# Talking-heads attention with a soft mixture of experts: raw logits and head mixing on sixteen 32x32 array tiles, rows brought together by SBUF-to-SBUF DMAs

## The chip, the cores and the metric

The kernel runs on one core of one Trainium2 chip. The metric is the time of one execution on the device, in microseconds (us). The time before is the median of three runs; the profile is that of one further execution. TensorE (PE in the profile) does matmuls out of SBUF into PSUM; VectorE (DVE) and ScalarE (ACT) read PSUM; GpSimd (POOL) works on SBUF alone; SyncE (SP) here only issues DMAs. PEld is TensorE's loading of weights.

## The reference

Input x is (4, 2048, 256), all in float32. For each of the 4 batches:

```
q, k, v = split(x @ Wqkv.T + bqkv)             # 16 heads of 16
q, k = rope(q), rope(k)
s = q @ k.T / 4                                # per head: raw logits, 2048 x 2048
l[g] = sum over h of Wpre[g, h] * s[h]         # the heads are mixed
a = softmax(l over keys)
t[g] = sum over h of Wpost[g, h] * a[h]        # and mixed again
x = layernorm(x + (t @ v) @ Wout.T + bout)
x = layernorm(x + soft_moe(x))                 # 16 experts of 16 slots, 64 hidden
```

Nearly all of the time lies in the four lines from s to t @ v.

## The kernel before

The batches follow one another. For each, `qkv(b)` projects the 16 token tiles of 128 tokens and leaves q and k transposed in `qT` and `kT` (128 partitions, 2 chunks of 8 heads x 16, 2048 tokens) and v as rows. Then `attention` runs, then `moe`.

`attention` takes queries in pairs of blocks: a block x is 8 tokens, so a row of logits (token, head) fills one of 128 partitions, and a pair n holds 16 tokens. There are 128 pairs per batch, 512 in all. Keys are taken in two halves j of 1024. The steps of a pair:

- `block_q` (L340) spreads q over the heads with a mask, on GpSimd: `qb`, one instruction per pair.
- `raw_bank` (L357) makes the raw logits s of a bank of PSUM (128 x 512) with matmuls of 128 rows by 32 columns, four side by side (L368), and has the bank copied to `raw` in SBUF by DVE or ACT (L375). There are four banks per half.
- `logits` (L377) mixes the heads with Wpre, on four 64x64 tiles of the array (L389), into two PSUM tiles l of 1024 columns, one per block.
- `top` (L400) reduces l to its negated maximum m on DVE (L402); `expo` (L406) makes e = exp(l + m) with its sum on ACT (L410).
- `weights` (L416) corrects for the two halves' maxima: f and z on GpSimd, a short exponential of f on ACT (L424), a reciprocal of z on DVE (L429), and the scaled Wpost w on GpSimd (L432).
- `mix` (L442), four per pair in the next step of the loop, multiplies e with w and so transposes it (t, L461) into two banks each, copied to `aT` (L470) by DVE and ACT.
- `values` (L477) multiplies with v (o, L485), and `finish` (L503) projects with Wout (pz, L509) for every 128 tokens.

The loop over n writes out by hand what is interleaved: in step n the l of pair n, the s of pair n + 1, the mixes of pair n - 1. Each engine works through its instructions in the program's order. On TensorE that is, per step: l of half 0, s of half 0, mixes 1 and 2, l of half 1, mixes 3 and 4, s of half 1, o. On ACT the second half's order is: exponential, two copies of mix 3, exponential, f, one copy of mix 4, two copies of s; on DVE: two reductions, m, the other copy of mix 4, reciprocal z, two copies of s.

[...] The pool `ps_l` holds two tiles l of two banks; the pool `ps_t` has four single banks, which s, t, o and pz take in turn, 17 of them per pair. A bank is free again when it has been copied out. In SBUF the tag `raw` has 5 buffers (of 4 KB per partition), `k1` 6, `x` 4.

## Time and profile before

| what | value |
|---|---|
| median of three runs | 10,239.89 us (10,237.3 to 10,248.01) |
| the profiled execution, its own time | 10,242.24 us |
| its span in the profile | 10,240.5 us |
| mean granted TensorE clock | 0.986 of full speed |
| s, L368: 32,768 passes of 512 columns | 3,739.1 us busy |
| l, L389: 16,384 passes of 512 columns | 2,070.1 us busy |
| t, L461: 131,072 passes of 64 columns | 2,183.9 us busy |
| o, L485: 65,536 passes of 64 columns | 1,018.0 us busy |
| m, L402 on DVE: 2,048 reductions of 1024 | 2,412.7 us busy |
| e, L410 on ACT: 2,048 exponentials of 1024 | 2,285.8 us busy |
| all DMA | 74.04 MB, 63,584 packets |

A matmul of float32 appears as two passes, each with its own weight load. Busy times of one engine overlap where array tiles run side by side, so that a mean duration is longer than the distance of two passes. The chain of work that ended last follows the end of the program back from what released each step to what released that; its shares tell where time was spent that nothing else hid. The views by time (timeline, chain in order of time) give the start in us from the start of the span, the length, the engine, the line and the tile; a bracket holds the idle time ahead and what ended it. "Idle before, releaser" in the groups is the same, summed.

### The profile page before, as it was taken

Reading aid. Unit: us, or ns where it says so; the run is one execution under the profiler, and the core shown is the slowest. Engines: PE = TensorE matmul, PEld = TensorE weight load, DVE = VectorE, ACT = ScalarE, POOL = GpSimd, SP = SyncE. Lnnn points to the kernel's source line nnn. Section 1 sums busy time; section 2 is a strip of 40 time slices with the busy share of each in tenths; the row PEclk is TensorE's granted clock in tenths of the full one; section 3 lists DMA queues with packets and bytes.
Section 4 is the critical chain, followed back from the end, with each engine's and each line's share of the span. In section 5 each row is a group of like instructions: output and inputs, shape, how many; then the busy total and the mean of one; then the engine's idle time right before and its main releaser. Section 6 shows DMA issues by size and latency. Waiting matters only on the chain.

```text
span 10240.5 us, 523545 instructions
## 1 busy us (share of the span) xinstructions
PE 9268.5 (91%) x248404; PEld 5008.8 (49%) x248404; DVE 5613.3 (55%) x9064; ACT 4995.1 (49%) x9766; POOL 1284.9 (13%) x3409
## 2 busy tenths in 40 slices
PE   8999999997899999999689999999968999999996
PEld 4445545444444445445444545444544444444454
DVE  5555555554555555555455555555545555555554
ACT  3555555553455555555345555555534555555553
POOL 2111111111211111111121111111112111111111
PEclk9999999998999999999899999999989999999998
DMA  0000000000000000000000000000000000000000
GB/s 23 5 5 5 4 5 5 5 4 17 19 5 5 5 4 5 5 5 4 17 19 5 5 5 4 5 5 5 4 17 18 5 5 5 4 5 5 4 4 18
DMA packets 63584, 74.04 MB, mean 7 GB/s; under 512 B 30080, under 2 KB 59904, under 8 KB 61440
## 3 DMA queue, kind: packets, MB, share of 16 engines
q8 instruction: 1946, 31.88, 1.3%
q1 hardware_dynamic: 26880, 25.18, 0.8%
q10 hardware_dynamic: 34560, 15.36, 0.6%
q14 instruction: 198, 1.62, 0.1%
HBM read 32.13 MB, written 8.39 MB: 4 GB/s over the span
## 4 chain that ended last, share of the span: by engine, by line
PE 80%; ACT 9%; DVE 8%; issue 2%; POOL 1%; ACTq 0%; DMA 0%; POOLq 0%; DVEq 0%
PE s L368 36%; PE l L389 19%; PE t L461 10%; PE o L485 9%; DVE m L402 6%; ACT e L410 5%; ACT aT L470 3%; PE pqk L289 1%; PE pz L509 1%; PE pf L680 1%; PE l_d L197 1%; PE o_d L236 1%; POOL xn L591 0%; PE pv L294 0%; POOL xn L592 0%
## 5 line engine op out<-in xcount | busy, mean ns | idle before, releaser
L368 PE MATMUL s<-kT,qb 128*32 128x512 f32 x32768 | 3739.1, 596 | 551.4 <-ACT aT L470 551.3
L402 DVE TENSOR_REDUCE m<-l 128x1 f32<-128x1024 f32 x2048 | 2412.7, 1220 | 1269.8 <-PE l L389 1269.8
L410 ACT ACTIVATE e<-l,m 128x1024 f32<-128x1024 f32 x2048 | 2285.8, 1121 | 1262.7 <-DVE m L402 1262.6
L375 ACT COPY raw<-s 128x512 f32<-128x512 f32 x2048 | 1211.7, 592 | 2809.0 <-PE s L368 2808.4
L461 PEld LDWEIGHTS t<-w,e 64*64 64x64 f32 x131072 | 2103.4, 135 | 754.0 <-issue 685.9
L368 PEld LDWEIGHTS s<-kT,qb 128*32 128x32 f32 x32768 | 966.7, 109 | 2886.8 <-issue 1797.2
L461 PE MATMUL t<-w,e 64*64 64x64 f32 x131072 | 2183.9, 219 | 43.0 <-issue 34.9
L389 PE MATMUL l<-raw,wmix_sb 64*64 64x512 f32 x16384 | 2070.1, 596 | 7.2 <-ACT e L410 3.6
L470 ACT COPY aT<-t 128x512 f32<-128x512 f32 x2560 | 1450.4, 589 | 396.2 <-PE t L461 395.8
L375 DVE COPY raw<-s 128x512 f32<-128x512 f32 x2048 | 1354.7, 681 | 350.3 <-PE s L368 349.6
L470 DVE COPY aT<-t 128x512 f32<-128x512 f32 x1536 | 1058.2, 689 | 338.2 <-PE t L461 338.0
L485 PEld LDWEIGHTS o<-aT,v 128*32 128x32 f32 x65536 | 997.0, 110 | 329.3 <-issue 176.8
L485 PE MATMUL o<-aT,v 128*32 128x64 f32 x65536 | 1018.0, 220 | 31.6 <-issue 26.5
L423 POOL TENSOR_TENSOR f<-m,m 128x4 f32<-128x4 f32 x512 | 101.6, 198 | 6568.8 <-DVE m L421 6568.8
L389 PEld LDWEIGHTS l<-raw,wmix_sb 64*64 64x64 f32 x16384 | 566.5, 133 | 679.6 <-issue 616.8
L429 DVE RECIPROCAL z<-z 128x2 f32<-128x2 f32 x512 | 85.1, 166 | 1081.5 <-POOL z L428 1081.5
L496 DVE COPY aoT<-o 128x32 f32<-128x32 f32 x512 | 98.1, 192 | 1005.9 <-PE o L485 1005.7
L410 ACT ACTIVATION_READ_ACCUMULATOR e<-l,m 128x1 f32 x2048 | 421.9, 206 | 0.0
L343 POOL TENSOR_TENSOR qb<-qT,hmask 128x256 f32<-128x256 f32 x512 | 313.6, 634 | 73.3 <-PE s L368 73.3
L432 POOL TENSOR_TENSOR w<-wblk_sb,f 128x256 f32<-128x256 f32 x512 | 313.7, 613 | 40.3 <-POOL f L430 0.5
L426 POOL TENSOR_TENSOR zf<-f,z 128x4 f32<-128x4 f32 x512 | 102.5, 200 | 987.2 <-ACT f L424 987.2
L315 POOL TENSOR_TENSOR s<-qk,wq 128x256 f32<-128x256 f32 x128 | 115.9, 924 | 478.4 <-DVE qk L299 478.4
(123 smaller groups left out, 2602.0 us busy)
## 6 DMA issues: line engine op xcount, KB each, us to landing
x<-in_x_dram SPq DMA_DIRECT2D x64, 128.0 KB
xr<-in_x_dram SPq DMA_DIRECT2D x64, 128.0 KB
out_dram<-y SPq DMA_DIRECT2D x16, 512.0 KB
wm<-in_w_dram ACTq DMA_DIRECT2D x8, 512.0 KB
wm<-in_w_dram ACTq DMA_DIRECT2D x4, 1024.0 KB
wq<-in_wqkvT_dram ACTq DMA_DIRECT2D x4, 768.0 KB
wq<-in_bqkv_dram ACTq DMA_DIRECT2D x4, 384.0 KB
wq<-in_rope_dram ACTq DMA_DIRECT2D x4, 256.0 KB
```

The lines of the kernel that those rows point to most:

```text
L315: nc.gpsimd.tensor_mul(s[:, :, a, :], qk[:, :, 1 - a, :], ss[a])
L343: nc.gpsimd.tensor_tensor(qb, qT[:, :, ts(n, 2 * IB)].unsqueeze(3).to_broadcast([P, KC, 2 * IB, HC]), hmask.unsqueeze(1).unsqueeze(1).to_b ...
L368: nc.tensor.matmul(pr[32 * c : 32 * (c + 1), :], qb[:, c % 2, i0 : i0 + IQ, :].rearrange("p i h -> p (i h)"), kT[:, c % 2, j0 : j0 + 512], ...
L375: eng(raws[n][j, u][:, ts(jj, 512)], pr)
L389: nc.tensor.matmul(pls[x][64 * u : 64 * (u + 1), n0 : n0 + 512], wmix_sb[64 * x : 64 * (x + 1), :], raws[n][j, u][64 * x : 64 * (x + 1), n ...
L402: nc.vector.tensor_reduce(s["m2"][:, x, j : j + 1], s["l", j][x], AX.X, ALU.max, negate=True)
L410: nc.scalar.activation(e, s["l", j][x], AF.Exp, bias=s["m2"][:, x, j : j + 1], accum_out=s["z2"][:, x, j : j + 1],)
L426: nc.gpsimd.tensor_tensor(zf, f, z2, ALU.mult)
L432: nc.gpsimd.tensor_tensor(w, wblk_sb.rearrange("p g i -> p (g i)").unsqueeze(1).to_broadcast([P, 4, HEADS * IQ]), f.rearrange("p x j -> p ...
L461: nc.tensor.matmul(pts[r][64 * c : 64 * (c + 1), a, :], e[rows, k0 : k0 + 64], s["w"][rows, 2 * x + j, :], start=True, stop=True,)
L470: engs[r](aT[grp][:, ts(j, HT), :, i0 : i0 + IQ], pts[r].rearrange("p a (g i) -> p a g i", i=IQ),)
L485: nc.tensor.matmul(po[32 * c : 32 * (c + 1)].rearrange("p a i -> p (a i)"), v[:, t, g0 * HD : (g0 + 2) * HD], at[:, t, g0 : g0 + 2, :].rea ...
```

## The change

The raw logits go to sixteen 32x32 tiles: a row group of 32 partitions of q and k holds two heads, four column groups take the four 256-key quarters of the half, so that each PSUM bank belongs to one row group and holds both chunks of heads. A row of the array's output is then no longer a (token, head) row of one key range: partitions hold 32 combinations of key quarter, block, token and head parity, and the free axis holds 8 head pairs by 256 keys. Eight DMAs per key half, each with 16 partitions as source and 128 as destination, bring this into rows (token, head), with tokens arranged so that Wpre is applied on sixteen 32x32 tiles as well, which lie on diagonals of the array. All four banks of a half are filled by one call, chunk by chunk, and copied after that. `qb` is made by seven smaller instructions. `y` takes over the room of `qT`, `uT` that of `kT`, and the x tiles have two buffers.

```diff
-    RAWS = 5
+    RAWS = 3
+    ROWS = 6
+    HP = HEADS // 2
+    QN = 256
...
-        xt = work.tile([P, D], F32, tag="x", name=f"{name}_{b}_{t}", bufs=4)
+        xt = work.tile([P, D], F32, tag="x", name=f"{name}_{b}_{t}", bufs=2)
...
-        def block_q(n):
-
-            qb = k1([P, KC, 2 * IB, HC], f"qb_{b}_{n}")
-            nc.gpsimd.tensor_tensor(
-                qb,
-                qT[:, :, ts(n, 2 * IB)].unsqueeze(3).to_broadcast([P, KC, 2 * IB, HC]),
-                hmask.unsqueeze(1).unsqueeze(1).to_broadcast([P, KC, 2 * IB, HC]),
-                ALU.mult,
-            )
+        def pair_q(n):
+            qb = k1([P, KC, 2, 2, 4, 2, 2], f"qb_{b}_{n}")
+            t, t0 = divmod(n * 2 * IB, P)
+            for g in range(2):
+                for x in range(2):
+                    d = 2 * x + g
+                    for s0, s1 in ((0, 4 - d), (4 - d, 4)):
+                        if s0 == s1:
+                            continue
+                        i0 = t0 + x * IB + (s0 + d) % 4 * 2
+                        i1 = i0 + (s1 - s0) * 2
+                        shape = [P, KC, i1 - i0, 2]
+                        nc.gpsimd.tensor_tensor(
+                            qb[:, :, g, x, s0:s1].rearrange("p c s i h -> p c (s i) h"),
+                            qT[:, t, :, i0:i1].unsqueeze(3).to_broadcast(shape),
+                            hmask.unsqueeze(1).unsqueeze(1).to_broadcast(shape),
+                            ALU.mult,
+                        )
             return qb
...
-        def raw_bank(n, j, k, eng):
-            u, jj = k % 2, k // 2
+        def raw_banks(n, j, engs):
             qb = raws[n]["qb"]
-            pr = ps_t.tile([P, 512], F32, tag="t", name=f"s_{b}_{n}_{j}_{k}")
-            j0 = j * HALF + jj * 512
-            for c in range(4):
-                i0 = IB * (c // 2) + IQ * u
-                nc.tensor.matmul(
-                    pr[32 * c : 32 * (c + 1), :],
-                    qb[:, c % 2, i0 : i0 + IQ, :].rearrange("p i h -> p (i h)"),
-                    kT[:, c % 2, j0 : j0 + 512],
-                    start=True,
-                    stop=True,
-                )
-            eng(raws[n][j, u][:, ts(jj, 512)], pr)
+            prs = [
+                ps_t.tile([P, KC, QN], F32, tag="t", name=f"s_{b}_{n}_{j}_{r}") for r in range(4)
+            ]
+            for c in range(KC):
+                for r in range(4):
+                    rows = slice(32 * r, 32 * (r + 1))
+                    for q in range(4):
+                        nc.tensor.matmul(
+                            prs[r][32 * q : 32 * (q + 1), c, :],
+                            qb[rows, c, q // 2].rearrange("p x s i h -> p (x s i h)"),
+                            kT[rows, c, j * HALF + q * QN : j * HALF + (q + 1) * QN],
+                            start=True,
+                            stop=True,
+                        )
+            raw = raws[n]["from", j].rearrange("p (c r) k -> p c r k", c=KC)
+            return [lambda r=r: engs[r](raw[:, :, r, :], prs[r]) for r in range(4)]
+
+        def raw_rows(n, j):
+            raw, rows = raws[n]["from", j], raws[n]["to", j]
+            for q in range(4):
+                for x in range(2):
+                    p0 = 32 * q + 16 * x
+                    nc.sync.dma_start(rows[x][:, ts(q, QN)], raw[p0 : p0 + 16])
...
-            for n0 in range(0, HALF, 512):
-                for u in range(2):
-                    for x in range(2):
+            for x in range(2):
+                for h in range(2):
+                    for q in range(4):
+                        c = (q + 2 * x + h) % 4
                         nc.tensor.matmul(
-                            pls[x][64 * u : 64 * (u + 1), n0 : n0 + 512],
-                            wmix_sb[64 * x : 64 * (x + 1), :],
-                            raws[n][j, u][64 * x : 64 * (x + 1), n0 : n0 + 512],
+                            pls[x][32 * c : 32 * (c + 1), ts(h, 512)],
+                            wmix_sb[32 * q : 32 * (q + 1), :],
+                            raws[n]["to", j][x][32 * q : 32 * (q + 1), ts(h, 512)],
                             start=True,
                             stop=True,
                         )
...
-        uT = seq.tile([P, KC, N], F32, tag="qT", name=f"uT_{b}")
+        uT = seq.tile([P, KC, N], F32, tag="kT", name=f"uT_{b}")
...
-        y = seq.tile([P, NT, D], F32, tag="y", name=f"y_{b}")
+        y = heads[0].rearrange("p t c i -> p t (c i)")
```

In the program that comes out of this, TensorE keeps its order of blocks. On ACT a step now reads: two exponentials, two copies of s, two copies of mixes 1 and 2; two exponentials, two copies of mix 3, f, one copy of mix 4, two copies of s. On DVE: two reductions, two copies of s, two copies of mixes 1 and 2; two reductions, m, reciprocal z, the copy of mix 4, two copies of s. GpSimd makes qb behind w, several pairs ahead where its buffers allow. SyncE issues the sixteen DMAs of a pair, eight after each half's copies, with the x loads of `finish` among them. The first copy of a half waits for the eight DMAs that read its `raw` buffer three halves earlier.

More of the change, by code (lines that the diff above doesn't have):

```diff
@@ L78, in row_const @@
         return t
-    wmix_sb = const.tile([P, IQ * HEADS], F32, tag="wmix", name="wmix_sb")
+    wmix_sb = const.tile([P, 2 * HEADS], F32, tag="wmix", name="wmix_sb")
     nc.gpsimd.memset(wmix_sb, 0.0)
-    wpre_h = wpre.rearrange("(h d) g -> h d g", d=HD)
-    for r in range(P // HC):
-        c, i = divmod(r % (KC * IQ), IQ)
+    wpre_h = wpre.rearrange("(r a d) g -> a r d g", a=2, d=HD)
+    for r in range(P // HP):
+        i, h = divmod(r % 4, 2)
         nc.scalar.dma_start(
-            wmix_sb[r * HC : (r + 1) * HC, i * HEADS : (i + 1) * HEADS],
-            wpre_h[c * HC : (c + 1) * HC, 0, :],
-        )
-    hmask = const.tile([P, HC], F32, tag="hmask", name="hmask")
-    nc.gpsimd.memset(hmask, 1.0)
-    nc.gpsimd.affine_select(
-        out=hmask, in_=hmask, compare_op=ALU.is_ge, fill=0.0,
-        base=0, pattern=[[-HD, HC]], channel_multiplier=1,
-    )
-    nc.gpsimd.affine_select(
-        out=hmask, in_=hmask, compare_op=ALU.is_ge, fill=0.0,
-        base=HD - 1, pattern=[[HD, HC]], channel_multiplier=-1,
-    )
+            wmix_sb[r * HP : (r + 1) * HP, i * HEADS : (i + 1) * HEADS], wpre_h[h, :, 0, :]
+        )
     wblk_sb = const.tile([P, HEADS, IQ], F32, tag="wblk", name="wblk_sb")
@@ L113 @@
     scale_sb = row_const(scale, 1, "scale_sb")
-    mu_sb = work.tile([P, KC, ES], F32, tag="raw", name="mu_sb", bufs=RAWS)
+    mu_sb = work.tile([P, KC, ES], F32, tag="rows", name="mu_sb", bufs=ROWS)
     nc.scalar.dma_start(mu_sb, mu.rearrange("(c p) e -> p c e", p=P))
@@ L143 @@
     nc.vector.tensor_reduce(odd1, odd4, AX.X, ALU.max)
+    hmask = const.tile([P, 2], F32, tag="hmask", name="hmask")
+    nc.vector.tensor_scalar(hmask[:, 0:1], odd1, -1.0, 1.0, ALU.mult, ALU.add)
+    nc.vector.tensor_copy(hmask[:, 1:2], odd1)
     odd = const.tile([P, GI], mybir.dt.int32, tag="odd", name="odd")
     nc.vector.tensor_copy(odd, odd1.to_broadcast([P, GI]))
-    sq = work.tile([P, KC, ES], F32, tag="raw", name="sq", bufs=RAWS)
+    sq = work.tile([P, KC, ES], F32, tag="rows", name="sq", bufs=ROWS)
     nc.vector.tensor_mul(sq, mu_sb, mu_sb)
@@ L179, in k2 @@
     def k2(shape, name):
-        return work.tile(shape, F32, tag="raw", name=name, bufs=RAWS)
+        return work.tile(shape, F32, tag="rows", name=name, bufs=ROWS)
     def evac(i, dst, src):
@@ L274, in qkv @@
         nc.scalar.dma_start(rope_sb, rope.rearrange("(t p) k -> p t k", p=P))
-        qT = seq.tile([P, KC, N], F32, tag="qT", name=f"qT_{b}")
+        qT = seq.tile([P, NT, KC, P], F32, tag="qT", name=f"qT_{b}")
         kT = seq.tile([P, KC, N], F32, tag="kT", name=f"kT_{b}")
@@ L322, in turn @@
                 nc.tensor.transpose(pr[:, c, :], r[:, ts(c, P)], ident)
-            nc.vector.tensor_copy(qT[:, :, ts(t, P)], pr[:, :KC, :])
+            nc.vector.tensor_copy(qT[:, t], pr[:, :KC, :])
             nc.scalar.copy(kT[:, :, ts(t, P)], pr[:, KC:, :])
@@ L338, in attention @@
         raws = {}
-        def block_q(n):
-            qb = k1([P, KC, 2 * IB, HC], f"qb_{b}_{n}")
-            nc.gpsimd.tensor_tensor(
-                qb,
-                qT[:, :, ts(n, 2 * IB)].unsqueeze(3).to_broadcast([P, KC, 2 * IB, HC]),
-                hmask.unsqueeze(1).unsqueeze(1).to_broadcast([P, KC, 2 * IB, HC]),
-                ALU.mult,
-            )
+        def pair_q(n):
[16 more added lines that the diff above has]
+                        )
             return qb
@@ L352, in raw_start @@
             if j == 0:
-                raws[n] = {"qb": block_q(n)}
-            for u in range(2):
-                raws[n][j, u] = work.tile([P, HALF], F32, tag="raw", name=f"raw_{b}_{n}_{j}_{u}", bufs=RAWS)
-        def raw_bank(n, j, k, eng):
-            u, jj = k % 2, k // 2
-            qb = raws[n]["qb"]
-            pr = ps_t.tile([P, 512], F32, tag="t", name=f"s_{b}_{n}_{j}_{k}")
-            j0 = j * HALF + jj * 512
-            for c in range(4):
-                i0 = IB * (c // 2) + IQ * u
-                nc.tensor.matmul(
-                    pr[32 * c : 32 * (c + 1), :],
-                    qb[:, c % 2, i0 : i0 + IQ, :].rearrange("p i h -> p (i h)"),
-                    kT[:, c % 2, j0 : j0 + 512],
-                    start=True,
-                    stop=True,
-                )
-            eng(raws[n][j, u][:, ts(jj, 512)], pr)
+                raws[n] = {"qb": pair_q(n)}
@@ new lines, in raw_start @@
+            raws[n]["from", j] = work.tile([P, HP, QN], F32, tag="raw", name=f"raw_{b}_{n}_{j}", bufs=RAWS)
+            raws[n]["to", j] = [
+                work.tile([P, HALF], F32, tag="rows", name=f"rows_{b}_{n}_{j}_{x}", bufs=ROWS)
+                for x in range(2)
+            ]
+        def raw_banks(n, j, engs):
+            qb = raws[n]["qb"]
+            prs = [
+                ps_t.tile([P, KC, QN], F32, tag="t", name=f"s_{b}_{n}_{j}_{r}") for r in range(4)
+            ]
+            for c in range(KC):
[11 more added lines that the diff above has]
+            return [lambda r=r: engs[r](raw[:, :, r, :], prs[r]) for r in range(4)]
@@ L385, in logits @@
             pls = [ps_l.tile([P, HALF], F32, tag="l", name=f"l_{b}_{n}_{j}_{x}") for x in range(2)]
-            for n0 in range(0, HALF, 512):
-                for u in range(2):
-                    for x in range(2):
+            for x in range(2):
+                for h in range(2):
+                    for q in range(4):
+                        c = (q + 2 * x + h) % 4
                         nc.tensor.matmul(
-                            pls[x][64 * u : 64 * (u + 1), n0 : n0 + 512],
-                            wmix_sb[64 * x : 64 * (x + 1), :],
-                            raws[n][j, u][64 * x : 64 * (x + 1), n0 : n0 + 512],
+                            pls[x][32 * c : 32 * (c + 1), ts(h, 512)],
+                            wmix_sb[32 * q : 32 * (q + 1), :],
+                            raws[n]["to", j][x][32 * q : 32 * (q + 1), ts(h, 512)],
                             start=True,
@@ L518, in attention @@
             raw_start(0, j)
-            for k in range(4):
-                raw_bank(0, j, k, (V, S_)[k % 2])
+            for f in raw_banks(0, j, (V, S_, V, S_)):
+                f()
+            raw_rows(0, j)
         for n in range(n_pairs + 3):
@@ L525, in attention @@
             val = 0 <= grp < N // GI
+            nop = [lambda: None] * 4
             for j in range(2):
@@ L531, in attention @@
                 if j == 0:
-                    if nxt:
-                        raw_bank(n + 1, j, 0, S_)
+                    fs = raw_banks(n + 1, j, (S_, V, S_, V)) if nxt else nop
+                    fs[0]()
                     if cur:
@@ L536, in attention @@
                         expo(n, j, 0)
-                    if nxt:
-                        raw_bank(n + 1, j, 1, V)
+                    fs[1]()
                     if cur:
                         top(n, j, 1)
-                    if nxt:
-                        raw_bank(n + 1, j, 2, S_)
+                    fs[2]()
                     if cur:
                         expo(n, j, 1)
+                    fs[3]()
                     if nxt:
-                        raw_bank(n + 1, j, 3, V)
+                        raw_rows(n + 1, j)
                     if prv:
@@ L562, in attention @@
                     if nxt:
-                        for k in range(4):
-                            raw_bank(n + 1, j, k, (V, S_)[k % 2])
+                        for f in raw_banks(n + 1, j, (V, S_, V, S_)):
+                            f()
+                        raw_rows(n + 1, j)
                     if val:
```

## The prediction

> **What bounds the kernel now.** I read the page first: its busy shares, then the chain of work that ended last.

> ```profile
> PE 9268.5 (91%) x248404; PEld 5008.8 (49%) x248404; DVE 5613.3 (55%) x9064; ACT 4995.1 (49%) x9766; POOL 1284.9 (13%) x3409
> PE 80%; ACT 9%; DVE 8%; issue 2%; POOL 1%; ACTq 0%; DMA 0%; POOLq 0%; DVEq 0%
> PE s L368 36%; PE l L389 19%; PE t L461 10%; PE o L485 9%; DVE m L402 6%; ACT e L410 5%; ACT aT L470 3%; PE pqk L289 1%; PE pz L509 1%; PE pf L680 1%; PE l_d L197 1%; PE o_d L236 1%; POOL xn L591 0%; PE pv L294 0%; POOL xn L592 0%
> ```

> TensorE looks like the bound, and the two kinds of matmul that the change speeds up (s and l) hold 55% of the chain. But 14% of it is m, e and aT, which are not TensorE's. So I read the chain over one pair in order of time (start, duration, what):

> ```profile
> 1319.54 3.64 PE s L368 x32
> 1323.18 1.79 PE o L485 x128
> 1324.97 1.88 PE l L389 x16
> 1326.85 3.57 PE s L368 x32
> 1330.42 2.03 PE t L461 x128
> 1332.44 1.79 PE l L389 x16
> 1334.23 1.22 DVE m L402
> ...
> 1335.54 1.08 ACT e L410
> ...
> 1336.64 0.59 ACT aT L470
> 1337.22 0.04 issue
> 1337.27 0.62 PE s L368
> ```

> A pair takes 1337.27 - 1319.54 = 17.73 us; 512 pairs are 9,078 us of the span. Of the pair, 14.7 us are TensorE's, and the end is a wait: s of the second key half needs PSUM banks that aT copies free. The other reductions, exponentials and copies lie beside the two s blocks of 3.6 us. That cover is what the change takes away. The timelines of DVE and of TensorE give lengths, and in the last line a gap of TensorE outside attention:

> ```profile
> 1321.76 0.17 DVE L429 RECIPROCAL z<-z 128x2 f32<-128x2 f32 x1 [2.12 <-POOL z L428]
> 1321.84 1.27 DVE L375 COPY raw<-s 128x512 f32<-128x512 f32 x2
> 1326.90 2.36 DVE L402 TENSOR_REDUCE m<-l 128x1 f32<-128x1024 f32 x2 [1.44 <-PE l L389]
> 2587.52 1.08 PE L322 MATMUL pr<-ident,r 128*128 128x128 f32 x4 [4.07 <-DVE r L316]
> ```

> **The change, part by part.** *TensorE.* Weight loads stand 0.43 us apart in l (PEld at 1325.38 and 1325.81), so a pass over 512 columns holds its tile 0.43 us, and 256 columns 0.21. Now s has 64 passes of 256 columns on 16 tiles: four deep, 0.85 us instead of 3.6. l has 32 passes of 512 on 16 tiles: two deep, 0.86 us instead of 1.8. Removed per pair: 2 x 2.75 + 2 x 0.95 = 7.4 us of TensorE. That 16 tiles run together no row shows (all here use four); bounds are 0.85 and, if only four do, 3.4 us for s. I take 0.9: four tiles do run fourfold now, and passes of o issue every 14 ns (128 in 1.79 us), so 64 need 0.9.

> If the rest stayed hidden, the pair would be near ACT's 4.5 + 0.8 + 2.4 + 2.8 + 0.2 = 10.7 us (e, its accumulator, raw, aT, f: busy sums over 512). It does not stay hidden. `raw_banks` takes all four banks of ps_t at once, with chunk c outermost: no bank is finished before the fourth is free, and none of the following mixes can start before s is copied out. And the scheduler orders the second half anew: ACT runs both exponentials before the copies of the third mix (before: one, copies, the other), and DVE takes the reciprocal z ahead of the fourth mix's copy (before: after it). So I lay the pair out by hand, from the start of l:

> - l, 0.86 with 0.17 to drain (596 less 427 ns) and the issue of 32 passes: 1.2.
> - Two reductions one after the other, 2.36: to 3.6. The second exponential, 1.1, and hops: to 4.9.
> - Behind it on ACT the copy of s bank 0, 0.59: to 5.5. Only now mixes 1 and 2, 2.02: to 7.5. s itself was done at 2.2: TensorE stood for 3.4 us.
> - l of the second half, 1.1: to 8.6. Two reductions, 2.4: to 11.0. The second exponential: to 12.2.
> - ACT: two copies of mix 3, 1.06, and f, 0.22: to 13.45. POOL: zf and z, 0.2 each with hops: to 13.95. DVE: z 0.17, then mix 4's copy, 0.69: to 14.8. Only now has s of the second half its last bank.
> - s 0.85: to 15.6; copy on DVE 0.69: to 16.3; o waits for that bank, 1.8, and two changes of tile shape with hops, 0.3: to 18.4.

> The hand sum is 18.4 us against 17.73, with 7.4 us less matmul: late next are the evacuations, in series.

> *The clock.* TensorE now stands from 2.2 to 5.6 and from 10.5 to about 12.8, and then works in drops until 14.8. What such gaps cost is seen in stretches of 3.41 us (second column the length, then PE, PEld, DVE, ACT, POOL busy, PEclk):

> ```profile
> 88.08:91.50 3.42, 0.56 (x5) 0.32 (x3) 1.43 (x3) 0.21 (x1) 3.42 (x5) 1.00 0.00 0
> 91.50:94.91 3.41, 1.73 (x8) 0.92 (x12) 1.45 (x3) 0.52 (x2) 0.81 (x2) 0.50 0.00 0
> 2583.23:2586.64 3.41, 0.22 (x2) 0.00 (x0) 3.41 (x11) 0.00 (x0) 0.00 (x0) 1.00 0.92 306
> 2586.64:2590.06 3.42, 2.08 (x7) 1.64 (x8) 3.14 (x7) 0.67 (x2) 1.85 (x2) 0.50 0.93 310
> 2648.08:2651.50 3.42, 0.41 (x4) 0.42 (x4) 1.03 (x2) 0.19 (x1) 2.14 (x4) 1.00 0.00 0
> 2651.50:2654.91 3.41, 3.41 (x18) 0.80 (x20) 1.12 (x2) 0.56 (x2) 0.00 (x0) 0.50 0.00 0
> ```

> Three stretches with 0.2 to 0.6 us of TensorE work, around gaps of 4.1 us, are each followed by one or two at half clock. [...] By the rows a mostly empty window is enough. A half-clock window full of matmuls loses 1.7 us: behind the first gap it falls on the mixes and l (1.7), behind the second on s and o (about 0.4 more on the path). I take the rows: 18.4 + 2.1 = 20.5, which is six windows, a length at which the pattern can repeat.

> *DMAs.* 16 per pair, 128 KB each, on SP's queue. SP spaces issues at 0.5 us (four x loads issued in 1.82 us, 0.33 each), so 8 us per pair. Moving 128 KB at the 306 GB/s of the row above is 0.43 us, 6.9 us per pair. Both fit in 18 us. The first half's rows are asked for at 6 and read at 18.4; the second's at 17 and read at 7.4 of the next pair, 8.8 us later: 4 us of issue and 2 to land fit. But each source is 16 partitions. No row here has that. [...] By the trace's rate DMA costs 0[...]. I keep both ends and put 0.2 into none. A wait here holds l, and behind it everything on TensorE. xr loads stand in the same queue, every eighth pair; POOL waits for them.

> *POOL.* qb becomes seven instructions: 7 x 0.19 (fixed part, from 198 ns for 4 elements) + 128 elements x 1.65 ns = 1.5 us instead of 0.63. POOL then has 2.9 us per pair and runs qb several pairs ahead: 0. Its cover gone, it would cost 0.9 per pair in front of f. *Copies* keep their number and size: 0. [...] *Batch ends:* qT now holds y, so the next batch's first turn waits for four stores of 512 KB (7 us at 306 GB/s), three times; two x buffers instead of four. I take 20 us in all, 0 to 60.

> **Sum.** 512 x (20.5 - 17.73) = +1,418, and 20: against this execution's own 10,242.2 (span 10,240.5), which lies 2 us above the median of the runs, 11,680; I say 11,660 on the median.

> **Rivals.** *Chain without clock loss:* 18.4 us, 10,242 + 343 + 20 = about 10,600. For it: the second gap is filled with drops of work, and dips of TensorE to half its share of a window elsewhere leave the clock alone. Against: the three rows. *DMA is the bound:* [...] For it: 1 GB in all through queues that now move 74 MB. [...] *Faster:* the wait for POOL's z, which DVE takes ahead of mix 4's copy, is not on the path (its row of before, 2.12 us of idle, cost nothing). Then the last bank is freed by ACT's copy of mix 4 at 14.0 instead of 14.8: 17.6 us, 10,195; with the 0.3 us that I put down for hops and tile shapes gone as well, 17.3 and 10,040. It decides at 14.1: with the last bank later than that the pair is over 17.73. For it: some hops are guessed. Against: the program's order on DVE is fixed, all lengths ahead of z are measured, and it needs a full clock. I see 0.1. *It doesn't do what it says:* only four tiles at once; s is 3.4 and sits on the chain (+2.6): 21 us, about 11,900; I count it with the first case's upper side.

> **How the numbers follow.** Chain with clock loss 0.5 (11,300 to 12,300), chain without 0.22 (10,400 to 11,200), DMA bound 0.15 (11,400 to 13,500), faster 0.10, no change 0.03. A measurement of this kernel can tell about 0.2%, 20 us. Slower is 0.5 + 0.22 + 0.15 = 0.87. From 10,560 to 12,800 lie all of the first case, nine tenths of the second and two thirds of the third: 0.8.

> **What would show it.** TensorE busy near 55 to 65%, not 91; s near 0.9 us and l near 1.1; idle TensorE ahead of t put down to ACT's raw copy and ahead of s to DVE's aT; z waiting for POOL ahead of aT; the granted clock clearly under 0.99. It is wrong if the clock stays at 0.99, if l waits for rows (then DMA), or if the pair is under 17.7.

## The result and the profile after

The changed kernel takes 12,032.18 us (median of four runs, 12,024.91 to 12,042.16) where the kernel before takes 10,241.1: a ratio of 1.175, 95% interval 1.1728 to 1.1769. The forecast was 11,660 in a range of 10,560 to 12,800, with 0.87 for slower. The profiled execution took 12,029.57 us, its span is 12,027.8. In the trace the mean distance from pair to pair went from 17.99 to 21.48 us (with the work of `finish` every eighth pair); its 508 distances within batches make 508 x 3.49 = 1,773 of the 1,787 us between the two spans.

The page first: busy times, instruction loads (queue, loads, MB, share), and the chain that ended last.

```profile
PE 9060.5 (75%) x297556; PEld 6135.0 (51%) x297556; DVE 5612.6 (47%) x9066; ACT 5105.5 (42%) x9766; POOL 1624.0 (14%) x6478
q8 instruction: 2346, 38.44, 1.3%
PE 29%; SPq 23%; DMA 19%; ACT 12%; DVE 7%; issue 7%; POOL 2%; ACTq 0%; POOLq 0%; DVEq 0%
```

TensorE fell from 91% to 75% busy, and the mean granted clock from 0.986 to 0.845. The chain puts 42% on SP and DMA (`SPq` is SP's issuing), which would be the DMA rival of the forecast. The first experiment below shows that this reading is wrong.

One pair in the timeline, from the start of its first l (start, length, what; in brackets the idle time ahead and what ended it): TensorE, then ACT, then DVE.

```profile
1346.64 1.33 PE L416 MATMUL l<-rows,wmix_sb 32*32 32x512 f32 x32
1347.52 1.76 PE L382 MATMUL s<-kT,qb 32*32 32x256 f32 x64
1352.11 3.00 PE L488 MATMUL t<-w,e 64*64 64x64 f32 x128 [2.83 <-ACT raw L390]
1355.05 1.86 PE L416 MATMUL l<-rows,wmix_sb 32*32 32x512 f32 x32
1356.83 2.36 PE L488 MATMUL t<-w,e 64*64 64x64 f32 x128
1361.08 1.70 PE L382 MATMUL s<-kT,qb 32*32 32x256 f32 x24 [1.89 <-ACT aT L497]
1363.02 2.00 PE L382 MATMUL s<-kT,qb 32*32 32x256 f32 x40 [0.23 <-DVE aT L497]
1364.94 2.78 PE L512 MATMUL o<-aT,v 128*32 128x64 f32 x128
...
1351.30 0.19 ACT L437 ACTIVATION_READ_ACCUMULATOR e<-l,m 128x1 f32 x1
1351.39 1.06 ACT L390 COPY raw<-s 128x512 f32<-128x512 f32 x2
1360.46 1.06 ACT L497 COPY aT<-t 128x512 f32<-128x512 f32 x2
...
1347.83 2.36 DVE L429 TENSOR_REDUCE m<-l 128x1 f32<-128x1024 f32 x2 [0.63 <-PE l L416]
1362.21 0.17 DVE L456 RECIPROCAL z<-z 128x2 f32<-128x2 f32 x1 [2.76 <-POOL z L455]
1362.29 0.67 DVE L497 COPY aT<-t 128x512 f32<-128x512 f32 x1
```

More than four tiles do run together: the 64 passes of s take 1.76 us with their drain, where four at a time would have taken 3.4 and more (16 turns of the forecast's 0.21). But TensorE then stands for 2.83 us ahead of t, until ACT has copied s behind its second exponential, and for 1.89 us ahead of s, until ACT and DVE have emptied t. The last s starts 0.06 us after DVE's copy, and that copy came right behind the reciprocal z, which had kept DVE idle for 2.76 us.

```profile
1349.58:1353.00 3.42, 0.89 (x60) 0.92 (x64) 1.80 (x3) 2.87 (x6) 0.00 (x0) 1.00 0.75 138
1353.00:1356.41 3.41, 3.41 (x115) 2.42 (x107) 1.38 (x2) 1.17 (x2) 0.00 (x0) 0.50 0.81 148
1356.41:1359.82 3.41, 2.78 (x146) 2.14 (x128) 2.52 (x3) 1.60 (x3) 0.20 (x1) 1.00 0.78 153
1359.82:1363.24 3.42, 1.93 (x40) 0.68 (x56) 0.75 (x2) 2.28 (x6) 1.10 (x4) 1.00 0.20 42
1363.24:1366.65 3.41, 3.41 (x104) 2.27 (x79) 1.29 (x2) 1.17 (x2) 0.11 (x1) 0.50 0.03 7
```

Each gap is followed by one stretch at half clock, in which the work that the gap had held back runs slower: t takes 3.00 us behind the first gap, most of it at half clock, and 2.36 in the second half at full clock. Over the whole trace 3,731 us ran at half clock, in the kernel before 290.

One thing is new. TensorE also stops in the middle of blocks of equal matmuls, where no instruction waits for anything (timeline of another pair):

```profile
1334.66 1.33 PE L416 MATMUL l<-rows,wmix_sb 32*32 32x512 f32 x20 [0.76 <-issue]
1339.42 0.57 PE L488 MATMUL t<-w,e 64*64 64x64 f32 x21 [1.67 <-issue]
```

The waits view (who waited for what, us in total, times, longest) has the idle time ahead of t; first the changed kernel, then the kernel before:

```profile
PE t L488 <- issue: 500.8, 437, 2.3
```

```profile
PE t L461 <- issue: 34.9, 67, 1.9
```

Idle time ahead of t that nothing but issue ended has grown from 35 to 501 us. I counted in the trace how often two neighbouring TensorE instructions of one block, the second without a wait, are issued over 0.7 us apart: 551 times (774 us together) in the changed kernel, 80 times (96 us) in the kernel before. Of the 551, 525 end 1.0 to 1.8 us after the end of a load on the instruction queue q8; loads are 5.1 us apart on the mean, so by chance it would be about one in six. Below these are "the stops".

### The profile page after: what moved, and what is told of

It reads as the page before. It is cut to its first block, busy times and chain, and to the rows that moved or that the text cites. A ratio compares the mean times of both kernels' runs of the same rounds, so it can differ in the third digit from the quotient of the medians.

```text
span 12027.8 us, 648378 instructions
## 1 busy us (share of the span) xinstructions
PE 9060.5 (75%) x297556; PEld 6135.0 (51%) x297556; DVE 5612.6 (47%) x9066; ACT 5105.5 (42%) x9766; POOL 1624.0 (14%) x6478
## 3 DMA queue, kind: packets, MB, share of 16 engines
q8 instruction: 2346, 38.44, 1.3%
## 4 chain that ended last, share of the span: by engine, by line
PE 29%; SPq 23%; DMA 19%; ACT 12%; DVE 7%; issue 7%; POOL 2%; ACTq 0%; POOLq 0%; DVEq 0%
SPq L398 23%; DMA rows<-raw 18%; PE s L382 10%; PE t L488 9%; ACT e L437 5%; ACT raw L390 4%; PE l L416 4%; ACT aT L497 3%; DVE m L429 2%; PE o L512 2%; DVE aT L497 2%; DVE raw L390 1%; PE pqk L284 1%; PE pf L709 1%; DMA xr<-in_x_dram 1%
## 5 line engine op out<-in xcount | busy, mean ns | idle before, releaser
L488 PE MATMUL t<-w,e 64*64 64x64 f32 x131072 | 2640.9, 240 | 1818.2 <-ACT raw L390 1303.3
L488 PEld LDWEIGHTS t<-w,e 64*64 64x64 f32 x131072 | 2433.6, 153 | 2641.5 <-issue 2145.2
L382 PE MATMUL s<-kT,qb 32*32 32x256 f32 x65536 | 2841.4, 437 | 621.4 <-ACT aT L497 489.8
L429 DVE TENSOR_REDUCE m<-l 128x1 f32<-128x1024 f32 x2048 | 2416.4, 1220 | 822.4 <-PE l L416 821.8
L382 PEld LDWEIGHTS s<-kT,qb 32*32 32x32 f32 x65536 | 1288.1, 109 | 1827.6 <-ACT aT L497 910.1
L416 PE MATMUL l<-rows,wmix_sb 32*32 32x512 f32 x32768 | 1724.3, 679 | 79.1 <-DMA rows<-raw 37.0
L512 PEld LDWEIGHTS o<-aT,v 128*32 128x32 f32 x65536 | 1510.0, 155 | 465.2 <-DVE raw L390 394.1
L512 PE MATMUL o<-aT,v 128*32 128x64 f32 x65536 | 1621.5, 285 | 97.8 <-issue 54.4
L390 ACT COPY raw<-s 128x512 f32<-128x512 f32 x2048 | 1132.4, 587 | 1142.8 <-PE s L382 1141.4
L351 POOL TENSOR_TENSOR qb<-qT,hmask 128x16 f32<-128x16 f32 (+3 forms) x3584 | 648.8, 220 | 285.5 <-PE s L382 285.5
L416 PEld LDWEIGHTS l<-rows,wmix_sb 32*32 32x32 f32 x32768 | 490.6, 113 | 360.3 <-issue 215.6
```

The costliest lines, as they stand in the source:

```text
L351: nc.gpsimd.tensor_tensor(qb[:, :, g, x, s0:s1].rearrange("p c s i h -> p c (s i) h"), qT[:, t, :, i0:i1].unsqueeze(3).to_broadcast(shape) ...
L382: nc.tensor.matmul(prs[r][32 * q : 32 * (q + 1), c, :], qb[rows, c, q // 2].rearrange("p x s i h -> p (x s i h)"), kT[rows, c, j * HALF + ...
L390: return [lambda r=r: engs[r](raw[:, :, r, :], prs[r]) for r in range(4)]
L416: nc.tensor.matmul(pls[x][32 * c : 32 * (c + 1), ts(h, 512)], wmix_sb[32 * q : 32 * (q + 1), :], raws[n]["to", j][x][32 * q : 32 * (q + 1) ...
L429: nc.vector.tensor_reduce(s["m2"][:, x, j : j + 1], s["l", j][x], AX.X, ALU.max, negate=True)
L488: nc.tensor.matmul(pts[r][64 * c : 64 * (c + 1), a, :], e[rows, k0 : k0 + 64], s["w"][rows, 2 * x + j, :], start=True, stop=True,)
```

## The experiments

Each time is the median of four runs. Twelve kernels, three questions: is it the order of evacuations (the copies out of PSUM), is it the clock, is it instructions or DMAs? Order means that in which ACT and DVE take up their instructions. Gains are against the changed kernel's 12,032 us unless another is named.

**no_dma.** The DMAs are left out, so l mixes rows of different tokens. ACT and DVE keep the changed kernel's order.

```diff
-                    nc.sync.dma_start(rows[x][:, ts(q, QN)], raw[p0 : p0 + 16])
+                    pass
...
-                            raws[n]["to", j][x][32 * q : 32 * (q + 1), ts(h, 512)],
+                            raws[n]["from", j].rearrange("p a k -> p (a k)")[
+                                32 * q : 32 * (q + 1), ts(2 * x + h, 512)
+                            ],
```

> The changed kernel without its 8,192 DMAs: the mixing with Wpre reads the copied raw logits where they lie, so the rows it mixes are not those of one token (that part of the computation is changed; sizes, copies and matmuls stay). Theory (evacuations in series, then the clock): rows land with time to spare, l waits for them 95 us in all, so the time stays within 150 us of 12,032. Rival (DMA bound, or DMA traffic holds up SP, the copies and TensorE's instruction loads): 1 us of DMA each, 16 per pair, is near the path, and without it the pair falls by 1 us or more: 11,500 or less, and TensorE's stops inside a block of equal matmuls go away.

11,906.13 us, ratio to before 1.1626 (1.1607 to 1.1645): 126 us less, 1%. The stops are 495 (507 us), not gone. So 1 GB of DMA cost this kernel 1%, although its chain holds SP and DMA with 42%. The chain of the changed kernel, in the pair shown:

```profile
1347.14 4.11 DMA rows<-raw
1351.24 0.05 issue
1351.30 0.19 ACT e L437
1351.49 0.49 ACT raw L390
```

Where the chain leaves the DMAs, it goes on with the end of an exponential and the copy of s behind it, which ACT works off without idle time: that copy waited for its own engine, and the last DMA to land was only an event ahead of it. The clock stayed as low (0.836).

**half1 and half2.** ACT and DVE are bound to a written order, in half1 for the first key half, in half2 for the second. `manual_schedule` makes an engine keep the order in which the instructions are written; `weights_end` is `weights` from the reciprocal z on. half2 also moves one copy of mix 4 from ACT to DVE, the second V of `(V, V)`. (Condensed: the comments are added; guards, the `raw_rows` calls and the lines replaced are left out.)

```diff
+ with tc.manual_schedule(engines={mybir.EngineType.Activation, mybir.EngineType.DVE}):
+     # half1 (j == 0)
+     top(n, j, 0); expo(n, j, 0); top(n, j, 1)
+     fs[0](); fs[1](); fs[2](); fs[3]()
+     expo(n, j, 1)
+     # half2 (j == 1)
+     top(n, j, 0); expo(n, j, 0); top(n, j, 1)
+     mix(n - 1, 1, 0, (S_, S_)); mix(n - 1, 1, 1, (V, V))
+     expo(n, j, 1); weights(n)
+     for f in raw_banks(n + 1, j, (V, S_, V, S_)):
+         f()
+     weights_end(n); values(grp, hf)
```

> The changed kernel with ACT and DVE bound to a written order in the first key half alone: ACT's two copies of s ahead of the second exponential. Chain theory: mixes 1 and 2 wait for those copies, which start 1.1 us earlier; DVE's copies then end last, so 0.7 to 1.1 us per pair less, 350 to 560 us, and a shorter first gap gives back some half-clock time: 11,200 to 11,650. Rival (taken back by stops in t, which then comes sooner, or by the exponential that now ends later ahead of l): less than 200 us less.

> The changed kernel with ACT and DVE bound to a written order in the second key half: copies of the third mix ahead of the second exponential on ACT, both copies of the fourth mix on DVE ahead of m and of the reciprocal z, z behind the raw copies. Chain theory: the last bank for s comes free about 2.4 us earlier (no second exponential, f or z ahead of it), 1,230 us less at equal clock and more if the gap that costs the clock closes too: 10,300 to 10,900. Rival (the period is set by something else: DMA, instruction supply or o): less than 500 us less.

half1: 11,314.81 us (1.1053, 1.1036 to 1.1069), 717 less, within the range expected; half-clock time fell to 2,816 us. half2: 11,451.88 us (1.1183, 1.1164 to 1.1201), 580 less, between what the theory and its rival gave. Both orders matter. But half2 brought less than half of its sum, and its TensorE shows why:

```profile
1350.20 1.49 PE L494 MATMUL t<-w,e 64*64 64x64 f32 x83
1353.32 0.92 PE L494 MATMUL t<-w,e 64*64 64x64 f32 x45 [1.63 <-issue]
1354.17 3.56 PE L382 MATMUL s<-kT,qb 32*32 32x256 f32 x64
```

With the copies earlier, s is hardly held by a bank any more (its idle time behind ACT's aT fell from 490 to 130 us), but the t ahead of it stops for 1.63 us in its middle; most of s follows at half clock. The stops rose from 551 (774 us) to 912 (1,232 us), in half1 to 783 (1,156 us).

**tuned.** Both orders together.

> The changed kernel with both orders written out, first half as in half1 and second half as in half2. The two gains lie in different gaps and add, less what the stops for instructions take: half2 gave 580 us, half1 is put at 450, so 10,800 to 11,200 if the stops grow as in half2 (1,232 us of issue gaps). If evacuation order were all that made the change slow, it would come to 10,200 or less, as fast as the kernel before.

10,971.22 us (1.0713, 1.0695 to 1.0731): 1,061 less than the changed kernel, four fifths of 717 + 580, and still 7% slower than before. The stops are 1,119 (1,635 us). So order is worth more than half of the 1,791 us, and is not all of it.

**t128.** A try at fewer instructions: t on two tiles of 64 rows by 128 columns in place of four of 64 by 64. (Condensed.)

```diff
-                    for c in range(2):
-                        k0 = a * P + 64 * c
-                        nc.tensor.matmul(
-                            pts[r][64 * c : 64 * (c + 1), a, :], e[rows, k0 : k0 + 64],
+                    nc.tensor.matmul(pts[r][:, a, :], e[rows, ts(a, P)],
```

> The changed kernel with t on two array tiles of 64 rows by 128 columns in place of four of 64 by 64: the same products, the same array time, but 256 fewer TensorE instructions of about 1,152 per pair. In the trace of the changed kernel TensorE stops 551 times for more than 0.7 us inside a block of equal matmuls with no wait, 774 us of issue gaps (80 times, 96 us, in the kernel before), 373 of them in t; 525 end 1.0 to 1.8 us after a 16 KB load on the instruction queue. Theory of instruction supply: loads fall from 2,346 to about 1,850, the stops in t mostly go, and the time falls by 300 to 600 us, to 11,430 to 11,730. Rival (these stops are hidden, or weight loads of 128 columns cost what they save): within 60 us of 12,032, or slower.

14,594.45 us (1.4261, 1.4212 to 1.4311): 2,562 slower. The premise of equal array time was wrong. In groups by line:

```profile
L486 PE MATMUL t<-w,e 64*128 64x64 f32 x65536 | 6573.2, 389 | 1257.5 <-ACT raw L390 1245.4
L486 PEld LDWEIGHTS t<-w,e 64*128 64x128 f32 x65536 | 6400.6, 299 | 2327.4 <-issue 2110.8
```

A block of t in a stretch of full clock takes 3.8 us, where the kernel before took 2.0, and in 3.65 of these 3.8 us a weight load is under way: at full clock a load of 128 columns takes 188 ns on the mean, one of 64 columns 135 in the changed kernel. The mean granted clock fell to 0.675, and DVE came out in another order (the copy of mix 4 ahead of z). As a test of instruction supply its time is worthless. Its loads and stops can be read: 1,834 loads instead of 2,346, and 149 stops (171 us) instead of 551, none of them in t, where 373 had been.

**half_instr.** Fewer instructions at the same tile shapes and the same number of columns; the products in s and o are then others.

```diff
-            for c in range(KC):
+            for c in range(1):
...
-                            prs[r][32 * q : 32 * (q + 1), c, :],
-                            qb[rows, c, q // 2].rearrange("p x s i h -> p (x s i h)"),
-                            kT[rows, c, j * HALF + q * QN : j * HALF + (q + 1) * QN],
+                            prs[r][32 * q : 32 * (q + 1)].rearrange("p c k -> p (c k)"),
+                            qb[rows, q % 2, q // 2].rearrange("p x s i h -> p (x s i h)"),
+                            kT[rows, q % 2, k0 : k0 + 2 * QN],
...
-            for t in range(NT):
+            for t in range(0, NT, 2):
...
-                        at[:, t, g0 : g0 + 2, :].rearrange("p a i -> p (a i)"),
+                        at[:, t, g0 & 12 : (g0 & 12) + 4, :].rearrange("p a i -> p (a i)"),
```

> The changed kernel with s in half as many matmuls of 512 columns and o in half as many of 128: the same columns on tiles of the same shape, so the same array time, but 256 fewer of 1,152 TensorE instructions per pair (the products are then of other columns: that part of the computation is changed; copies, DMAs and waits stay). Supply theory: t's 512 instructions per pair still come in a burst, but loads fall to about 1,850 and the stops to under half (under 390 us of issue gaps); the time falls by 300 to 800 us, to 11,230 to 11,730. Rival (the stops are hidden behind the evacuations): within 100 us of 12,032.

11,550.59 us (1.1285, 1.1268 to 1.1301): 482 less, in the expected range, although half-clock time rose to 4,103 us. Loads fell to 1,834 as expected, but the stops, counted as above, did not fall under half: they are some 790 (some 800 us). Of these, 480 lie in s, whose passes have 512 columns here, and only 107 of the 480 follow a load by 1.0 to 1.8 us. TensorE's idle time within the stops, a better measure here, went from 604 to 327 us.

The gain is not that of instructions alone, though. ACT came out in another order in the first half, with one copy of s between the two exponentials:

```profile
1342.74 1.11 ACT L438 ACTIVATE e<-l,m 128x1024 f32<-128x1024 f32 x1 [6.13 <-DVE m L430]
...
1343.85 0.58 ACT L391 COPY raw<-s 128x512 f32<-128x512 f32 x1
1344.31 1.13 ACT L438 ACTIVATE e<-l,m 128x1024 f32<-128x1024 f32 x1
...
1345.41 0.59 ACT L391 COPY raw<-s 128x512 f32<-128x512 f32 x1
```

It is so in every pair, and is part of what half1 does by hand. The idle time of t behind ACT's raw copies fell from 1,303 to 1,051 us, about as much as that of the stops. Without the loop over c each bank of s is also finished before the next is begun, so that its copy can start earlier. This run does not separate the three.

**tuned_half.** tuned and half_instr together; here the order on ACT and DVE is bound in both kernels compared.

> tuned and half_instr together (other products in s and o, as there). If order and instruction supply between them hold the period, the stops fall under half of those of tuned and the time falls by more than half_instr alone saves: 9,600 to 10,300, at or under the kernel before. If the DMAs (16 of about 1 us each) then bound the period, it stops at 16.5 to 17.5 us per pair, 9,500 to 10,100, with l waiting for rows. Rival (clock loss dominates whatever the order): over 10,700.

9,957.71 us (0.9718, 0.97 to 0.9737), under the kernel before, though with other products. Its chain by engine:

```profile
PE 40%; DMA 17%; SPq 14%; ACT 8%; issue 8%; DVE 5%; POOL 2%; ACTq 0%; DVEq 0%; POOLq 0%
```

On top of the mended order the same cut in instructions is worth 1,013 us. The stops fall from 1,119 to 504 (678 us), and the idle time ahead of t, s, o and l that nothing but issue ended from 1,337 to 480 us, 857 less: with the evacuations out of the way, instruction supply was the largest thing that held TensorE. Banks that are finished one by one remain a rival for a small part: o's wait for DVE's raw copies fell by 68 us.

**th_nodma and th_wide.** tuned_half without its DMAs, and tuned_half with the same bytes and packets from 128 partitions.

```diff
-                    nc.sync.dma_start(rows[x][:, ts(q, QN)], raw[p0 : p0 + 16])
+                    nc.sync.dma_start(rows[x][:, ts(q, QN)], raw[:, 2 * q + x])
```

> tuned_half without its 8,192 DMAs, l reading the copied raw logits where they lie (other products, as in no_dma and half_instr). If the DMAs bound tuned_half (their issue on SP takes 0.8 us each, 12.8 us of a pair, and its chain holds them with 30%), the time falls by 300 to 1,000 us, to 8,950 to 9,650. If they are still hidden: within 150 us of 9,958.

> tuned_half with each of its DMAs reading 1 KB of all 128 partitions in place of 8 KB of 16: the same bytes, packets and issues, from all of SBUF (other rows). If the source of 16 partitions limits the DMAs, packets (83 ns on the mean) get shorter by a third or more and rows land earlier; the time goes down as far as th_nodma shows it can, 100 to 800 us. Rival (issue on SP or the writes limit them): packets and time stay within 2% of tuned_half.

th_nodma: 9,075.59 us (0.8859, 0.8845 to 0.8874), 882 less than tuned_half. th_wide: 9,475.77 us (0.9256, 0.924 to 0.9271), 482 less, with packets of 1 KB at 47 ns on the mean instead of 83. The chain of tuned_half holds DMA with 17% and SP with 14%, and this time they count: what cost 1% in the changed kernel costs 9% once the rest is out of the way, and more than half of that goes with the source of 16 partitions.

**filler and tuned_filler.** More TensorE work in the first gap, in the changed kernel and in tuned.

```diff
+            for r in range(2 if j == 0 else 0):
+                nc.tensor.matmul(
+                    prs[r].rearrange("p c k -> p (c k)"), ident, kT[:, r, :512], start=True, stop=True
+                )
```

> The changed kernel with two more matmuls (128x128 by 512 columns, float32) ahead of the raw logits of each first key half, into banks that these then overwrite: 1.7 us more TensorE work per pair, put where TensorE otherwise idles. Clock theory: the first gap of a pair (2.8 us) shrinks to about 1.2, windows under half busy become fewer, half-clock time falls from 3,731 us to under 2,500, and with more work the time falls by 300 to 900 us, to 11,100 to 11,700. Rival (the clock loss lies off the path, or work in one gap does not keep the clock): same or up to 450 us slower.

> tuned with the two further matmuls of filler ahead of the first half's s. Half-clock time is 2,091 us there, worth 1,045 us at most. Clock theory: it falls to under 1,400 and the time by 150 to 400 us, to 10,570 to 10,820. Rival (with the order mended the gap is short, and the further work pushes s and its copies back, or what holds the kernel now is instruction supply alone): 10,970 to 11,300.

filler: 11,677.73 us (1.1403, 1.1386 to 1.142). Work was added (1,029.6 us of busy TensorE on that line) and the time fell by 354 us; half-clock time went from 3,731 to 2,492 us. This is the clock theory at work. tuned_filler: 11,285.74 us (1.1019, 1.0998 to 1.104), 315 slower than tuned, so there its rival was right: half-clock time fell only from 2,091 to 1,784 us. The traces show the difference. The filler makes the first half's s end 1.7 to 1.8 us later in both. In the changed kernel t starts no later for it, 5.8 us behind the start of l with and without; in tuned it starts 5.7 us behind l instead of 4.7.

**before_order.** The kernel before with its order mended and nothing else. Both halves are bound; the first keeps the order in which it was written. (Guards and removed lines are left out.)

```diff
+ with tc.manual_schedule(engines={mybir.EngineType.Activation, mybir.EngineType.DVE}):
...
+     # second key half
+     mix(n - 1, 1, 0, (S_, S_))
+     top(n, j, 0)
+     mix(n - 1, 1, 1, (V, S_))
+     top(n, j, 1)
+     expo(n, j, 0); expo(n, j, 1); weights(n)
+     for k in range(4):
+         raw_bank(n + 1, j, k, (V, S_)[k % 2])
+     weights_end(n); values(grp, hf)
```

> The kernel before (no sixteen tiles, no DMAs) with ACT and DVE bound to a written order: in the second key half ACT copies the third mix's two banks ahead of both exponentials, DVE has its copy of the fourth mix between the two reductions, z comes behind the raw copies. In the chain of the kernel before, m 1.22, e 1.08 and aT 0.59 us stand between l and the first s of the second half; without m and e ahead of the copy some 1.2 to 2 us of the 17.73 go: 9,300 to 9,700. Rival (TensorE at 91% is the bound there and the order only shifts waits): within 1% of 10,241.

9,719.96 us (0.9494, 0.948 to 0.9508): 5.1% under the kernel before, just outside the range expected, and the fastest kernel here that computes the whole of the reference. Its chain over a pair, in order of time:

```profile
1320.14 1.79 PE o L491 x128
1321.92 1.88 PE l L389 x16
1323.80 3.57 PE s L368 x32
1327.37 2.04 PE t L467 x128
1329.41 1.72 PE l L389 x16
1331.13 1.83 PE t L467 x125
1332.97 0.39 issue
1333.36 0.33 PE t L467 x3
1333.68 3.57 PE s L368 x32
```

m, e and aT, which stood between l and s in the chain of before, are gone. TensorE is busy 96% of the span at a clock of 0.984. With fewer instructions and longer passes the loads keep up here: 110 stops, 120 us.

This bears on the account of the change. tuned and before_order are the two kernels with their orders mended, and they lie 1,251 us apart, where the two without lie 1,791 apart. As far as the two mendings are alike, order explains some 540 us of what the change cost, and most of the rest came with the small tiles: instruction supply and a lower clock (0.905 against 0.984).

## Why the prediction was right, point by point

*The hand-laid chain.* From the start of l in the pair shown (1346.64):

| step | forecast, us | measured, us |
|---|---|---|
| second reduction done | 3.6 | 3.6 |
| second exponential done | 4.9 | 4.9 |
| mixes 1 and 2 start | 5.5 | 5.5 |
| mixes done, at full clock | 7.5 | 8.5, at half clock |
| l of the second half issued | 8.6 | 10.2 |
| reductions done | 11.0 | 12.6 |
| second exponential done | 12.2 | 13.9 |
| DVE's copy of mix 4 done | 14.8 | 16.3 |
| o done | 18.4 | 21.1 |

The first three steps hold to a tenth. The 0.3 us put down for two changes of tile shape agrees with the trace of before, where the first pass of l (64*64) mostly starts 0.149 us after the last of o (128*32), while passes of o follow each other every 14 ns. The order on each engine, read from the program, and durations from the trace of before were enough for that. The named waits (t for ACT's raw copies, s for DVE's aT behind z) are there, and half1, half2 and tuned show that they are causes: with both orders mended 1,061 us are gone.

*The clock.* Forecast: 1.7 us lost on the mixes and l, 0.4 on s and o, 2.1 a pair. Measured in this pair: l is issued 10.2 - 8.6 = 1.6 late; s and o take 21.1 - 16.3 = 4.8 us instead of 18.4 - 14.8 = 3.6, 1.2 lost. The second term was three times too small: the half-clock stretch from 1363.24 to 1366.65 covers most of s and o, not only their end. What the three rows of before pointed to can now be counted, over the stretches of 3.41 us of the whole trace. All 265 stretches at full clock in which TensorE was busy under 40% were followed by half clock; of those between 40 and 80%, 403 of 1,310; of those above 80%, 64 of 849. None of the 74 stretches at half clock with less than 70% busy was followed by full clock. So in this trace a mostly empty stretch was enough, as in the three rows of before: in the pair shown the gaps are 2.83 and 1.89 us, shorter than a stretch, and the two stretches hold 0.89 and 1.93 us of TensorE's work. The pair did not settle at six stretches (20.5 us), as the forecast thought possible; the mean is 21.48.

*What was not in the sum.* The forecast had 20.5 us a pair and 20 us at the batch ends: 1,438 in all, against 1,791. The batch ends took about 14 (span less distances, above). The other 0.7 us a pair must come from what the sum put too low or left out: the second clock term (0.8 us in the pair shown) and the stops, for which it had no term (TensorE's idle time in them rose from 51 to 604 us, 1.1 us a pair, a part of it beside waits). No run splits the two, since a stop also takes work out of its stretch, and the emptier stretches were the ones more often followed by half clock (the counts above). That 11,660 came within some 3% although instruction supply was not thought of is in part luck: in the changed kernel the series of evacuations still hid a part of what supply costs, and tuned_half shows that it was no small term.

*The signs named beforehand.* The two idle times of TensorE, the wait of z and the fall of the clock came as named. Two signs did not: TensorE is busy 75%, not 55 to 65, of which half clock is a part (o, with its passes unchanged, went from 1,018.0 to 1,621.5 us busy); and the 64 passes of s need 1.4 us to be issued at full clock, one every 22 ns, not 0.9. In the first half that is hidden; in the second it lies on the path. l, with 1.33 us for 1.1, was nearer.

*DMA.* The forecast put in 0.2 us per pair; no_dma says 0.25 (126 / 512). The upper end of that cost and the times of the DMA rival were the author's estimate, and no run shows a rate behind them. The issue on SP was mis-sized: 0.77 us each on the mean and 0.8 apart, not 0.5, so 12.8 us of SP per pair. It fitted in 21.5 us. Rows of eight DMAs landed mostly 8 to 9 us after their first issue, about 1 us each, over twice the 0.43 that the 306 GB/s of before had given. The rival's cost showed as soon as the pair got short: in tuned_half, at 17.4 us a pair ((9,958 - 12,032) / 512 + 21.48), the DMAs are on the path.

*The rivals.* The chain without clock loss did not come: the clock fell. "Faster, since z is not on the path" is refuted by the time itself, and in the pair shown the last s starts behind the copy that z held up; half2 gains, but moves z, the copies of mixes 3 and 4 and the second exponential together, so it gives no price for z alone. "Only four tiles at once" is refuted by the 1.76 us of s.

*POOL.* qb's seven instructions take 648.8 us / 512 = 1.3 us per pair, forecast 1.5, and TensorE's s waits for them 1.2 us in all.

## What to carry to other kernels

A busiest engine at 91% does not mean that making its matmuls faster saves their time: look at what lies beside them, lay the new period out by hand in each engine's program order, and see which copy frees the last bank. Here taking matmul time away (7.4 us a pair by the forecast) saved nothing, while the order of exponentials and copies alone was worth 2 us a pair (1,061 / 512); mending it in the kernel before gave 5% without the change. When an experiment changes the program, look whether the engines still work in the old order: half_instr was meant to change instructions only. Before a chain that names DMAs is believed, leave them out once: 42% of a chain was 1% of the time, and later, after other causes were reduced, 31% of a chain was 9%.

## What the hardware showed that was not expected

TensorE's instructions come in loads of 16 KB on q8 (38.44 MB / 2,346), one for 2 x 297,556 / 2,346 = 254 matmuls and weight loads. In the changed kernel two loads never start less than 3.27 us apart (3.28 in the kernel before), and only one in twenty less than 3.5. A load takes 1.0 us, and a stop ends some 1.4 us after it. If some 3.4 us, close to these least distances, is what can be kept up, 1,152 matmuls and weight loads per pair, 4.5 loads, need some 15.4 us whatever the array does (an estimate from these distances), and the 256 instructions of a block of t, which the kernel before issued in 1.9 us, use a load up faster than the next one comes. Smaller tiles doubled the passes of s (64 to 128 a pair) and l (32 to 64), and the stops went from 80 to 551.

Busy TensorE is not always enough for the clock: in t128 TensorE was busy 88%, yet of 2,672 stretches at half clock with over 80% busy 2,103 were followed by another. What separates the two outcomes far better in these traces is how much of the array works. Take for every pass started in a stretch its tile's rows times columns times its moving columns, and divide the sum by what 128 x 128 would take in 3.41 us at the 512 columns per 0.427 us of the kernel before. Over all fourteen traces, of 24,257 stretches at full clock with a share of 0.40 or more, one was followed by half clock; of 5,699 with less than 0.30, 4,940 were. Of the stretches at half clock, 4,412 of 4,422 with 0.40 or more were followed by full clock, and 89 of 3,907 with less than 0.30. This is counted, not tested by a run made for it, but it fits t128, whose blocks are busy with weight loads, and the filler, which uses the whole array.

It also shows what the change did to the clock beside its gaps. On tiles of 32 rows s no longer multiplies most of the zeros of the masked q. By the same measure that leaves a quarter of the array's work in s (64 x 128 x 32 x 512 before, 128 x 32 x 32 x 256 now) and half of it in l, and the mean share of the whole program fell from 0.82 to 0.41, to the edge of what held full clock here.
